# Layer-1 mixture of experts: dense blocks replaced by 79 sorted blocks filled and read back by indirect DMA

## The chip, the core and the metric

The kernel runs on one core of one Trainium2 chip. The metric is the device time of one execution in microseconds, the median of several. PE is the matrix engine, PEld its weight loads, DVE the vector engine, ACT the scalar engine, POOL is GpSimd and SP the engine that issues most DMAs.

## The reference

Two layers act on x, two sequences of 1024 tokens of 128 float32 features. Each layer normalizes x and adds attention and a mixture of experts (MoE), both of the normalized tokens, to x. Layer 0 has sigmoid attention and 32 experts of width 64. Layer 1 has softmax attention with relative positions, 16 heads of 8, and 16 experts of width 176, of which each token uses four, plus a shared expert of width 352:

```python
topk_idx, topk_w = _gate(x, gate_w, gate_bias)
combine_w = (jax.nn.one_hot(topk_idx, E, dtype=x.dtype) * topk_w[..., None]).sum(1)
g = jnp.einsum('th,eih->tei', x, gate_proj)
u = jnp.einsum('th,eih->tei', x, up_proj)
act = jax.nn.silu(g) * u
y = jnp.einsum('tei,ehi,te->th', act, down_proj, combine_w)
sg = x @ shared_gate_w.T
su = x @ shared_up_w.T
y = y + jax.nn.silu(sg) * su @ shared_down_w.T
```

The gate takes a sigmoid of 16 logits, keeps two of four groups of experts, then the four best experts, and normalizes their scores to sum to one. The sum over experts may therefore be taken over all sixteen with zero weights, or over the four chosen ones alone.

## The kernel before

Everything is float32. Tokens are handled in tiles of 128 (NT = 8 a sequence) and in blocks of 512 (TB).

**Layer 0** is a loop over c = 0 to 95 (N_ATT): each step makes the scores of one key tile (scores0, L413) and the weighted values of the step before (values0, L442), and between them opens and closes one FFN unit (open_unit L311, close_unit L336). A unit is 128 hidden rows for 512 tokens: two matmuls into PSUM (L319, L320), a sigmoid on ACT (L325), two multiplications on DVE (L326, L327), one on POOL (L333) by the combine weights of the rows' experts, which SP has spread over the partitions from a DRAM tensor (cb, L317, three buffers), and a third matmul (L345) that adds to the block's output. Every expert is computed for every token.

**Layer 1's FFN** (blocks1, L520) has the same form: 22 units of routed experts (M1 = 16 x 176 / 128) and three of the shared expert for each of four token blocks, 100 units, in the steps from c = 96 on. The gates (gate1, L489) run piecewise on DVE, that of sequence 0 within layer 0 and that of sequence 1 at c = 107 to 124. folded1 (L512) adds a finished block to x2s, the running x. Under these units lies the start of layer 1's attention: projections (L574), operands (L594), the first positions (L613) and ten scans (L652), spread over the steps c = 136 to 190 (L861). SP also writes the zero rows of the bounce tensors there (L558).

**Layer 1's attention** is a loop over 128 steps t: 16 groups of 8, a group being a sequence, a set of heads (s) and a block of 512 queries (q). A step computes scores and exp for one key tile (L705, L730), the values of the step before (L733), and a scan for a step LEAD = 10 ahead, which finds the row maxima that the scores need: four matmul row groups into four PSUM banks, reduced on DVE (L683, L688). positions(n, pair) makes the relative-position terms of two query tiles: matmuls (L624), copies on ACT (L627) and POOL (L629), a write to DRAM (L636) and a skewed read back (near, L642). It is called at step 8n - 13 or 8n - 9, three steps before its first scan. PE's order is the order of the program; POOL's and SP's instructions stand in their queues in the order in which they are issued, and one that waits holds those behind it. After a sequence's last group, finish (L757) and project (L768) write the output.

Of the kernel before, what the change touches and what calls it, by code (L numbers as in the profile page):

```python
# [19 lines left out]
B = 2  # L20
# [14 lines left out]
M1 = E1 * I1 // P  # L35
SH1 = 2 * I1
W = 512
# [5 lines left out]
def fused_layers_kernel(ctx: ExitStack, tc: tile.TileContext, a: dict, out: bass.AP):  # L43
# [13 lines left out]
    const = ctx.enter_context(tc.tile_pool(name="const", bufs=1))  # L57
    moe_pool = tc.tile_pool(name="moe", bufs=2, side="right")
# [28 lines left out]
    w1_pool = tc.tile_pool(name="w1pool", bufs=1, side="right")  # L87
    l1w = w1_pool.__enter__()
# [3 lines left out]
    def load(pool, name, shape, src=None):  # L92
        t = pool.tile(shape, F32, tag=name, name=name)
        nc.sync.dma_start(t, a[name] if src is None else src)
        return t
# [26 lines left out]
    gproj = load(l1w, "gproj", [P, E1 * I1])  # L122
    uproj = load(l1w, "uproj", [P, E1 * I1])
    dproj = load(l1w, "dproj", [P, M1, D], a["dproj"].rearrange("(m p) d -> p m d", p=P))
    sgw = load(l1w, "sgw", [P, SH1])
    suw = load(l1w, "suw", [P, SH1])
    sdw = l1w.tile([P, 3, D], F32, tag="sdw", name="sdw")
# [68 lines left out]

    def layernorm(x, xn, pool):
# [38 lines left out]
    def top_k(work, n_rows, n, k, pool, tag):  # L236

        picked = pool.tile([P, n_rows, n], F32, tag=tag + "p", name=tag + "p")
# [3 lines left out]
        for j in range(k):  # L242
# [6 lines left out]
            if j == 0:  # L249
                one = picked  # L250
            else:
                one = pool.tile([P, n_rows, n], F32, tag=tag + "o", name=tag + "o")
            nc.vector.tensor_tensor(one, eq, spread(best, n), ALU.is_equal)
            if j:
# [102 lines left out]
    cw1_rows = dram.tile([E1, B * T], F32, tag="cw1", name="cw1")  # L357
# [106 lines left out]
    def merged0(b):  # L464
# [6 lines left out]
        xn1[b] = l0.tile([P, T], F32, tag=f"xn{b}", name="xn1")  # L471
# [7 lines left out]
    def rows1(m):  # L479
        lo, end = m * P, (m + 1) * P  # L480
        got = []
        while lo < end:
            e = lo // I1
            hi = min(end, (e + 1) * I1)
            got.append((lo - m * P, hi - m * P, cw1_rows[e]))
            lo = hi
        return got

    def gate1(b):  # L489
# [11 lines left out]
        picked = yield from top_k(sf, NT, E1, K1, l1w, "e1")  # L501
        nc.vector.tensor_mul(picked, picked, sc)
        nc.vector.tensor_reduce(red, picked, AX.X, ALU.add)
        nc.vector.tensor_scalar(red, red, 1e-20, None, ALU.add)
        nc.vector.reciprocal(red, red)
        nc.vector.tensor_tensor(picked, picked, spread(red, E1), ALU.mult)
        yield
        combine_weights_out(picked, E1, l1w, cw1_rows, b)
# [11 lines left out]
    def blocks1(b):  # L520
        parts = [
# [478 lines left out]
```

## Time and profile before

| | |
|---|---|
| median of 3 runs | 1390.44 us (1388.61 to 1393.4) |
| the profiled execution's own time | 1393.02 us |
| its span | 1391.2 us, granted clock 0.987 |
| layer 0, 0 to 433.3 us | 433.3 us |
| layer 1's FFN and the attention's start, to 750.5 us | 317.2 us |
| layer 1's attention, 128 steps, to the end | 640.7 us |
| DMA over the span | 155.71 MB, mean 112 GB/s |

The span runs from the first instruction to the last. Busy time is summed by engine; a group of instructions is listed by line, engine, operation and tile names, with count, busy time, mean ns of one, and the idle time ahead of them with what ended it. A float32 matmul shows as two rows. The queue of a DMA-issuing engine, such as SP's, is not counted as busy.

### The profile page before, as it was taken

How to read it: one execution, taken by the hardware profiler on the slowest of the kernel's cores; microseconds unless marked ns; L12 is line 12 of the kernel's file. 1: busy time of each engine (PE TensorE's matmuls, PEld its weight loads, DVE VectorE, ACT ScalarE, POOL GpSimd, SP SyncE). 2: the span in 40 equal slices, each digit the busy share in tenths (PEclk: the TensorE clock that was granted, in tenths of full speed). 3: DMA queues.
4: the chain of work that ended last, by engine and by line, in shares of the span. 5: the costliest groups of instructions: out<-in, count | busy, mean ns of one | idle time of the engine just before them, and what ended most of it. 6: DMA issues, size and time to landing. Idle time of an engine off the chain costs nothing.

```text
span 1391.2 us, 21725 instructions
## 1 busy us (share of the span) xinstructions
PE 1300.9 (94%) x8080; PEld 548.6 (39%) x8080; DVE 802.5 (58%) x2111; ACT 613.2 (44%) x1051; POOL 290.9 (21%) x323
## 2 busy tenths in 40 slices
PE   5889999989999999989999999999999999999997
PEld 2323233323333434434434444443544444344443
DVE  7863343653334875646674665666567666666653
ACT  3534444535552222222213555555454454555554
POOL 0124243233333434343231001010000100010000
PEclk9999999999999999999999999999999999999999
DMA  8111111111111343255341555535544544554420
GB/s 274 37 43 58 49 58 46 39 38 41 46 52 55 106 114 100 61 173 154 112 131 57 163 158 182 173 125 159 166 136 161 161 165 137 183 160 141 155 92 16
DMA packets 107146, 155.71 MB, mean 112 GB/s; under 512 B 14464, under 2 KB 85760, under 8 KB 106528
## 3 DMA queue, kind: packets, MB, share of 16 engines
q1 hardware_dynamic: 107040, 154.32, 35.5%
q8 instruction: 64, 1.05, 0.3%
q14 instruction: 42, 0.34, 0.1%
HBM read 99.91 MB, written 54.37 MB: 111 GB/s over the span
## 4 chain that ended last, share of the span: by engine, by line
PE 70%; DVE 17%; DMA 5%; ACT 4%; issue 3%; POOL 1%; SPq 0%; DVEq 0%; POOLq 0%; ACTq 0%
PE big L319 10%; PE sm L724 10%; PE big L320 9%; PE ffn L345 8%; PE acc L741 8%; PE sm L663 8%; PE sm L714 5%; PE big L425 4%; PE acc L451 4%; DVE maxima L688 3%; DMA near<-bounce 3%; DVE junk L683 2%; DMA bounce<-rel 2%; DVE h L327 1%; DVE t L326 1%
## 5 line engine op out<-in xcount | busy, mean ns | idle before, releaser
L730 ACT ACTIVATE p<-sm 128x512 f32<-128x512 f32 x512 | 264.7, 606 | 234.0 <-PE sm L724 233.9
L688 DVE TENSOR_REDUCE maxima<-sm 128x1 f32<-128x512 f32 (+3 forms) x472 | 226.5, 502 | 123.0 <-PE sm L663 123.0
L333 POOL TENSOR_TENSOR h<-h,cb 128x512 f32<-128x512 f32 x152 | 193.6, 1274 | 378.9 <-DVE h L331 194.6
L431 ACT ACTIVATE at<-big 128x1024 f32<-128x1024 f32 (+1 forms) x192 | 144.9, 808 | 149.4 <-PE big L425 143.4
L683 DVE CUSTOM_DVE_ANT_0 junk<-sm,near 128x384 f32<-128x384 f32 (+2 forms) x292 | 130.4, 447 | 67.2 <-PE sm L663 53.6
L325 ACT ACTIVATE sg<-big 128x512 f32<-128x512 f32 (+1 forms) x100 | 59.7, 597 | 226.9 <-PE big L320 224.9
L629 POOL COPY rel<-rel 128x512 f32<-128x512 f32 x64 | 37.5, 614 | 537.5 <-ACT rel L627 537.5
L741 PE MATMUL acc<-p,vs 128*32 128x512 f32 (+1 forms) x1288 | 144.6, 518 | 0.4 <-ACT yu L753 0.4
L330 DVE SCALAR_TENSOR_TENSOR t<-big,b,sg 128x512 f32<-128x512 f32 x64 | 47.9, 749 | 157.7 <-ACT sg L329 157.7
L714 PE MATMUL sm<-ident,near 128*128 128x128 f32 x704 | 107.5, 284 | 21.2 <-DVE maxima L683 12.6
L326 DVE TENSOR_TENSOR t<-big,sg 128x512 f32<-128x512 f32 (+1 forms) x100 | 68.9, 689 | 92.0 <-ACT sg L325 91.9
L724 PE MATMUL sm<-qa,kls 32*128 32x512 f32 (+3 forms) x832 | 116.9, 545 | 0.0
L663 PE MATMUL sm<-kls,qs 32*128 32x512 f32 (+2 forms) x776 | 105.0, 569 | 1.2 <-ACT p L730 1.2
L714 PEld LDWEIGHTS sm<-ident,near 128*128 128x128 f32 x704 | 76.8, 142 | 70.9 <-issue 20.0
L425 PE MATMUL big<-qm,xT 32*128 32x512 f32 (+3 forms) x768 | 101.6, 544 | 3.1 <-ACT at L431 1.9
L345 PE MATMUL ffn<-h,dproj 128*128 128x512 f32 x176 | 91.9, 604 | 11.2 <-POOL h L333 11.2
L319 PE MATMUL big<-xT,gproj 128*128 128x512 f32 x176 | 92.3, 606 | 4.4 <-DVE h L327 3.5
L320 PE MATMUL big<-xT,uproj 128*128 128x512 f32 x176 | 90.3, 595 | 0.0
L451 PE MATMUL acc<-at,xn 128*32 128x512 f32 (+3 forms) x768 | 83.9, 510 | 6.5 <-POOL at L436 4.6
L319 PE MATMUL big<-xT,w 128*128 128x512 f32 x128 | 75.2, 670 | 14.9 <-DVE h L331 12.5
L627 ACT COPY rel<-sm 128x512 f32<-128x512 f32 x116 | 59.5, 600 | 50.5 <-issue 49.5
L327 DVE TENSOR_TENSOR h<-big,t 128x512 f32<-128x512 f32 (+1 forms) x100 | 69.1, 691 | 9.3 <-DVE t L326 0.9
(232 smaller groups left out, 1419.8 us busy)
## 6 DMA issues: line engine op xcount, KB each, us to landing
bounce<-rel SPq DMA_DIRECT2D x64, 768.0 KB
near<-bounce SPq DMA_DIRECT2D x64, 768.0 KB
cb<-cw SPq DMA_DIRECT2D x144, 128.0 KB
cb<-cw SPq DMA_DIRECT2D x32, 256.0 KB
cb<-cw SPq DMA_DIRECT2D x16, 224.0 KB
cb<-cw SPq DMA_DIRECT2D x16, 192.0 KB
cb<-cw SPq DMA_DIRECT2D x16, 160.0 KB
bounce<-zeros SPq DMA_DIRECT2D x40, 63.5 KB
```

Of the source, the lines that this page charges most:

```text
L319: nc.tensor.matmul(hh[0:m, 0, :], wa, xT, start=True, stop=True)
L320: nc.tensor.matmul(hh[0:m, 1, :], wb, xT, start=True, stop=True)
L333: nc.gpsimd.tensor_mul(h[0:m], h[0:m], cb[0:m])
L345: nc.tensor.matmul(y, w2m, h[0:m], start=first, stop=last and bias_mm is None)
L425: nc.tensor.matmul(halves[r // 2][:, r % 2, off:TB], xT0[b][g, kt * P:(kt + 1) * P], masked[b, s][g, q * TB + off:(q + 1) * TB], start=Tru ...
L663: nc.tensor.matmul(ps[r][:, (k0 - lo) * P:(k1 - lo) * P], qs[g, qt * P:(qt + 1) * P], (kh if far else kl)[g, k0 * P:k1 * P], start=True, s ...
L683: nc.vector.tensor_tensor_reduce(junk[:, 0:(k1 - k0) * P], part, near[n, i][:, r, w0:w0 + (k1 - k0) * P], 1.0, -BIG, ALU.add, ALU.max, mx[ ...
L688: nc.vector.tensor_reduce(mx[:, r, slot:slot + 1], part, AX.X, ALU.max)
L714: nc.tensor.matmul(ps[r][:, i * P:(i + 1) * P], near[n, i][:, r, w0:w0 + P], ident, is_transpose=True, start=(i == close[0]), stop=False, ...
L724: nc.tensor.matmul(ps[r][:, i0 * P:i1 * P], k[g, kt * P:(kt + 1) * P], qa[n][g, i0 * P:i1 * P], start=(m == 0 and not close), stop=(m == l ...
L730: nc.scalar.activation(p[:, r, :], ps[r], AF.Exp)
L741: nc.tensor.matmul(y[rows_of(r), part], vs[:, kt, rows_of(r)], probs[n, kt][:, r, part], start=(kt == 0), stop=(kt == NT - 1 and part.stop ...
```

## The change

The routed experts of layer 1 are no longer computed for every token. M1's units are gone from blocks1, which keeps the three shared units per block, and the loop of layer 0 ends 22 steps after step 96, with the attention's start in its last 16 steps.

Instead, top_k now hands out each of the four choices by itself (chosen), gate1 keeps the four weights (share), and sort1 gives each token and choice a slot: the tokens of one expert take whole blocks of 128 slots, in the order of the experts, NBLK = 79 blocks in all, which hold any routing of 2048 x 4 choices. It also lists for each block the rows of its expert's weights. gate1 of sequence 1 and sort1 run piecewise in the attention's steps 1 to 25.

Three DRAM tensors are new: slots_x and slots_y (the blocks' inputs and outputs, 79 x 128 rows of 512 B) and wx (for each expert 128 rows of 608 floats: the gate, up and down weights of both halves of its 176 hidden rows). In layer 0's steps 30 to 72 SP writes the bounce tensors' zero rows (moved here), zeros into slots_x (clear) and wx (regroup); gproj, uproj and dproj are no longer loaded to SBUF.

In steps 26 to 57 POOL issues 64 scatters, two a step: 128 normalized tokens each, to their slots. Ahead of step 64, when sequence 0's scores are done, all 79 blocks run on PE (experts): SP fetches four blocks of tokens at a time, PE turns them, POOL gathers each block's weights by an indirect DMA into a ring of six buffers, and hidden and outputs are two blocks apart. In steps 65 to 96 POOL issues 64 gathers of outputs, two a step, and DVE adds each, times its weight, into x2s two steps later. The positions due at step 63 are moved behind the experts, to step 64. The ring of near tiles shrinks from 12 to 10, the output is written from x2s, and project adds into it.

```diff
 SH1 = 2 * I1
+I1H = I1 // 2
+WX = 4 * I1H + 2 * D
+
+NBLK = (B * T * K1 + E1 * (P - 1)) // P
+NTT = B * NT
...
-    gproj = load(l1w, "gproj", [P, E1 * I1])
-    uproj = load(l1w, "uproj", [P, E1 * I1])
-    dproj = load(l1w, "dproj", [P, M1, D], a["dproj"].rearrange("(m p) d -> p m d", p=P))
-    sgw = load(l1w, "sgw", [P, SH1])
...
-            if j == 0:
+            if each:
+                one = each[j]
+            elif j == 0:
...
-    cw1_rows = dram.tile([E1, B * T], F32, tag="cw1", name="cw1")
+    slots_x = dram.tile([NBLK * P, D], F32, tag="slots_x", name="slots_x")
+    wx = dram.tile([E1 * P, WX], F32, tag="wx", name="wx")
+    slots_y = dram.tile([NBLK * P, D], F32, tag="slots_y", name="slots_y")
...
-        xn1[b] = l0.tile([P, T], F32, tag=f"xn{b}", name="xn1")
+        xn1[b] = const.tile([P, T], F32, tag=f"xn1{b}", name="xn1")
...
-        nc.vector.tensor_reduce(red, picked, AX.X, ALU.add)
+        mine = slice(b * NT, (b + 1) * NT)
+        yield from top_k(sf, NT, E1, K1, l1w, "e1", [t[:, mine, :] for t in chosen])
+        for j in range(K1):
+            nc.vector.tensor_mul(sf, chosen[j][:, mine, :], sc)
+            nc.vector.tensor_reduce(share[:, mine, j], sf, AX.X, ALU.add)
+            yield
+        nc.vector.tensor_reduce(red, share[:, mine, :], AX.X, ALU.add)
...
+        nc.vector.tensor_tensor(share[:, mine, :], share[:, mine, :], spread(red, K1), ALU.mult)
...
+        nc.vector.tensor_add(some, chosen[0], chosen[1])
+        nc.vector.tensor_add(some, some, chosen[2])
...
+        nc.vector.tensor_add(some, some, chosen[3])
+        ps = small()
+        rank, in_tile = (ps[:, i * NTT * E1:(i + 1) * NTT * E1] for i in range(2))
+        nc.tensor.matmul(rank, ahead, flat[0], start=True, stop=True)
+        nc.tensor.matmul(in_tile, ones, flat[0], start=True, stop=True)
...
+        nc.vector.tensor_copy(some, in_tile)
+        nc.vector.memset(at[:, 0, :], 0.0)
+        for t in range(1, NTT):
+            if t % 8 == 1:
+                yield
+            nc.vector.tensor_add(at[:, t, :], at[:, t - 1, :], some[:, t - 1, :])
+        nc.vector.tensor_add(n_tok, at[:, NTT - 1, :], some[:, NTT - 1, :])
...
+        nc.vector.tensor_add(at, at, rank)
...
+        nc.vector.tensor_tensor(some, spread(n_tok, NTT), filled.unsqueeze(1).to_broadcast(by_e), ALU.is_gt)
+        nc.vector.tensor_reduce(n_blk, some, AX.X, ALU.add)
...
+        nc.vector.tensor_tensor(some, lower, n_blk.unsqueeze(1).to_broadcast(by_e), ALU.mult)
+        nc.vector.tensor_reduce(start_, some, AX.X, ALU.add)
+        nc.vector.tensor_add(end_, start_, n_blk)
+        nc.vector.tensor_scalar(start_, start_, float(P), None, ALU.mult)
...
+        nc.vector.tensor_tensor(at, at, start_.unsqueeze(1).to_broadcast(wide), ALU.add)
+        for j in range(K1):
+            nc.vector.tensor_mul(some, chosen[j], at)
+            nc.vector.tensor_reduce(slot[:, :, j], some, AX.X, ALU.add)
+            yield
+        nc.vector.tensor_copy(slot_of, slot)
+        row = l1w.tile([P, NBLK], F32, tag="row", name="row")
+        for lo in range(0, NBLK, NTT):
+            n = min(NTT, NBLK - lo)
+            nos = block_no[:, lo:lo + n]
+            nc.vector.tensor_tensor(some[:, 0:n, :], end_.unsqueeze(1).to_broadcast([P, n, E1]),
+                                    spread(nos, E1), ALU.is_le)
+            nc.vector.tensor_reduce(row[:, lo:lo + n], some[:, 0:n, :], AX.X, ALU.add)
+            yield
+        nc.vector.tensor_scalar(row, row, float(E1 - 1), float(P), ALU.min, ALU.mult)
+        nc.vector.tensor_scalar(row, row, row_no, None, ALU.add)
+        nc.vector.tensor_copy(weight_row, row)
...
+    def clear(i):
+
+        n = min(4, NBLK - 4 * i)
+        nc.sync.dma_start(slots_x[4 * i * P:(4 * i + n) * P, :].rearrange("(i p) d -> p i d", p=P),
+                          zeros.unsqueeze(1).to_broadcast([P, n, D]))
...
+    def regroup(i):
+
+
+        by_row = wx.rearrange("(e p) w -> p e w", p=P)
+        if i < 2:
+            nc.sync.dma_start(by_row[:, :, i * I1:(i + 1) * I1],
+                              a[("gproj", "uproj")[i]].rearrange("p (e w) -> p e w", e=E1))
+        else:
+            c = slice(2 * I1 + (i - 2) * D, 2 * I1 + (i - 1) * D)
+            nc.sync.dma_start(wx.rearrange("(e p) w -> e p w", p=P)[:, 0:I1H, c],
+                              a["dproj"].rearrange("(e j p) d -> j e p d", j=2, p=I1H)[i - 2])
+            nc.sync.dma_start(by_row[I1H:P, :, c], zeros[I1H:P].unsqueeze(1).to_broadcast([P - I1H, E1, D]))
...
+    def scatter(i):
+
+        t, j = i // K1, i % K1
+        x = xn1[t // NT][:, (t % NT) * D:(t % NT + 1) * D]
+        nc.gpsimd.indirect_dma_start(
+            slots_x[:, :], bass.IndirectOffsetOnAxis(ap=slot_of[:, t, j:j + 1], axis=0), x, None
+        )
...
+    def gather(i):
+
+        t, j = i // K1, i % K1
+        y = pools["late"].tile([P, D], F32, tag="got", name="got", bufs=6)
+        nc.gpsimd.indirect_dma_start(
+            y, None, slots_y[:, :], bass.IndirectOffsetOnAxis(ap=slot_of[:, t, j:j + 1], axis=0)
+        )
+        fetched[i] = y
+
+    def gathered(i):
+        t, j = i // K1, i % K1
+        x = x2s[t // NT][:, t % NT, :]
+        nc.vector.scalar_tensor_tensor(x, fetched.pop(i), share[:, t, j:j + 1], x, ALU.mult, ALU.add)
+        if t < NT and j == K1 - 1 and t % 4 == 3:
+            result(0, t // 4)
+
+    def result(b, q):
+        nc.sync.dma_start(out[b, q * TB:(q + 1) * TB, :].rearrange("(i p) d -> p i d", p=P),
+                          x2s[b][:, 4 * q:4 * q + 4, :])
+
...
+    def fetch_w(i):
+        if i >= NBLK:
+            return
+        if i % 6 < 4:
+            t = const.tile([P, T], F32, tag=("xn10", "xn11", "xT10", "xT11")[i % 6], name="blockw")
+        else:
+            t = pools["late"].tile([P, 2 * T], F32, tag="p", name="blockw", bufs=2)
+        nc.gpsimd.indirect_dma_start(
+            t[:, 0:WX], None, wx[:, :], bass.IndirectOffsetOnAxis(ap=weight_row[:, i:i + 1], axis=0)
+        )
+        block_w[i] = t
+
+    def fetch_x(g):
+        if 4 * g >= NBLK:
+            return
+        n = min(4, NBLK - 4 * g)
+        t = held["room"][:, g % 2]
+        nc.sync.dma_start(
+            t[:, 0:n, :], slots_x[4 * g * P:(4 * g + n) * P, :].rearrange("(i p) d -> p i d", p=P)
+        )
+        block_x[g] = t
...
+    def turn_x(g):
+        if 4 * g >= NBLK:
+            return
+        n = min(4, NBLK - 4 * g)
+        ps = quads(small())
+        x = block_x.pop(g)
+        for i in range(n):
+            nc.tensor.transpose(ps[:, i, :], x[:, i, :], ident)
+        t = held["room"][:, 2 + g % 2]
+        nc.scalar.copy(t[:, 0:n, :], ps[:, 0:n, :])
+        block_xT[g] = t
+
+    def hidden(i):
+
+        w, xT = block_w[i], block_xT[i // 4][:, i % 4, :]
+        ps = quads(small())[0:I1H]
+        for j in range(4):
+            nc.tensor.matmul(ps[:, j, :], w[:, j * I1H:(j + 1) * I1H], xT, start=True, stop=True)
+        sg = w[0:I1H, WX:WX + 2 * P].rearrange("p (i c) -> p i c", c=P)
+        h = pools["late"].tile([P, 2, P], F32, tag="bh", name="bh", bufs=3)[0:I1H]
+        nc.scalar.activation(sg, ps[:, 0:2, :], AF.Sigmoid)
+        nc.vector.tensor_mul(sg, ps[:, 0:2, :], sg)
+        nc.vector.tensor_mul(h, ps[:, 2:4, :], sg)
+        block_h[i] = h
...
+    def outputs(i):
+        g, n = i // 4, min(4, NBLK - i // 4 * 4)
+        if i % 4 == 0:
+            block_y[g] = quads(small())
+        ps, h, w = block_y[g], block_h.pop(i), block_w.pop(i)
+        for j in range(2):
+            c = 4 * I1H + j * D
+            nc.tensor.matmul(ps[:, i % 4, :], h[:, j, :], w[0:I1H, c:c + D], start=(j == 0), stop=(j == 1))
+        if i % 4 == n - 1:
+            t = held["room"][:, 4 + g % 2]
+            nc.scalar.copy(t[:, 0:n, :], ps[:, 0:n, :])
+            nc.sync.dma_start(
+                slots_y[4 * g * P:(4 * g + n) * P, :].rearrange("(i p) d -> p i d", p=P), t[:, 0:n, :]
+            )
...
+    def experts():
+
+        held["room"] = pools["l1"].tile([P, 2 * NG * NEAR], F32, tag="rel", name="room").rearrange(
+            "p (k i c) -> p k i c", k=6, c=D)
+        for g in range(2):
+            fetch_x(g)
+        turn_x(0)
+        for i in range(NBLK + 2):
+            if i < NBLK:
+                hidden(i)
+            if i >= 2:
+                outputs(i - 2)
+                fetch_w(i + 4)
+            if i % 4 == 1:
+                turn_x(i // 4 + 1)
+                fetch_x(i // 4 + 2)
...
     def blocks1(b):
-        parts = [
-            (P, gproj[:, m * P:(m + 1) * P], uproj[:, m * P:(m + 1) * P], dproj[:, m, :], None, None,
-             rows1(m)) for m in range(M1)
-        ]
+        parts = []
...
-            slot = 4 * (n % 3) + 2 * pair + j
+            slot = (4 * n + 2 * pair + j) % 10
...
-        nc.vector.tensor_add(o, x2s[b][:, 4 * q:4 * q + 4, :], ps)
-        nc.sync.dma_start(out[b, q * TB:(q + 1) * TB, :].rearrange("(i p) d -> p i d", p=P), o)
+        x = x2s[b][:, 4 * q:4 * q + 4, :]
+        nc.vector.tensor_add(x, x, ps)
+        if b:
+            result(b, q)
...
+    for i in range(N_BOUNCE):
+        at(30 + i, bounce_rows, i)
+    for i in range(-(-NBLK // 4)):
+        at(30 + N_BOUNCE + i, clear, i)
+    for i in range(4):
+        at(60 + 4 * i, regroup, i)
...
     at(N_ATT, blocks1, 0)
     at(N_ATT + 2, added0, 1)
...
+    at(N_ATT + 5, lambda: l0_pool.__exit__(None, None, None))
+    at(N_ATT + 5, opened1)
+    at(N_ATT + 9, turned1, 1)
+    at(N_ATT + 9, blocks1, 1)
+    LAST = N_ATT + 22
...
-                at(N_ATT + 40 + (t - min(begin)) * 58 // -min(begin), f, *args)
+                at(LAST + t * (LAST - N_ATT - 6) // -min(begin), f, *args)
...
+    SORT, SCATTER, EXPERTS = 1, 26, 8 * len(groups) // B
...
+    def routing():
+        yield from gate1(1)
+        yield from sort1()
...
+    for t in range(SORT, SCATTER - 1):
+        for i in range(1 + t % 2):
+            beside(t, route_on)
+    beside(SCATTER - 1, route_on, True)
+    for i in range(NTT * K1):
+        beside(SCATTER + i // 2, scatter, i)
+        beside(EXPERTS + 1 + i // 2, gather, i)
+        beside(EXPERTS + 3 + i // 2, gathered, i)
+    for i in range(4):
+        beside(EXPERTS - 1, fetch_w, i)
...
         for t in range(N_STEPS + 1):
+            if t == EXPERTS:
+                values(t // 8 - 1, NT - 1, whole)
+                for i in range(4, 6):
+                    fetch_w(i)
+                experts()
             before = begin.get(t, ())
+            if t == EXPERTS:
+                before = list(before) + held_back
+            elif t == EXPERTS - 1:
+                held_back = [e for e in before if e[0] is positions]
+                before = [e for e in before if e[0] is not positions]
...
-            if t:
+            if t and t != EXPERTS:
                 values(n, kt, left if halved else whole)
...
+            for f, args in aside.get(t, ()):
+                f(*args)
```

## The prediction

> **What bounds the kernel now.** I read the page's first two parts, then the busy time by stage, the groups of the second stage, PE's timeline, the waits and the chain. The profiled execution took 1393.02 us, its span is 1391.2 us, and the median shown is 1390.44 us; the sum below is made on the span: 1.8 us lie around it, and this execution is 2.6 us above the median, so 0.8 us come off at the end.
>
> ```profile
> PE 1300.9 (94%) x8080; PEld 548.6 (39%) x8080; DVE 802.5 (58%) x2111; ACT 613.2 (44%) x1051; POOL 290.9 (21%) x323
> ```
>
> PE is busy nearly throughout. The stages, cut at the first layer-1 expert matmul (433.3), the first attention score of layer 1 (750.5), the middle of that attention and the end (columns: us, then busy us of PE, PEld, DVE, ACT, POOL, clock, DMA share, GB/s):
>
> ```profile
> 0.00:433.30 433.30, 395.91 (x2041) 132.73 (x2042) 208.06 (x486) 203.74 (x277) 128.04 (x138) 0.98 0.20 64
> 433.30:750.50 317.20, 298.59 (x860) 130.31 (x858) 204.60 (x408) 74.19 (x125) 121.76 (x115) 0.99 0.38 110
> 750.50:1070.50 320.00, 306.04 (x2592) 144.70 (x2596) 198.05 (x625) 168.15 (x325) 22.36 (x38) 0.99 0.49 158
> 1070.50:1391.20 320.70, 300.35 (x2592) 140.82 (x2584) 191.76 (x593) 167.17 (x325) 18.78 (x32) 0.98 0.41 133
> ```
>
> The change empties the second row and puts new work at the third row's end. A step of the attention is 640.7/128 = 5.0 us, PE-bound, with DVE at 62% and POOL at 7%. The expert groups of the second row, and how closely PE packs such matmuls:
>
> ```profile
> L319 PE MATMUL big<-xT,gproj 128*128 128x512 f32 x176 | 92.3, 606 | 4.4 <-DVE h L327 3.5 <-DVE maxima L683 0.9
> L345 PE MATMUL ffn<-h,dproj 128*128 128x512 f32 x176 | 91.9, 604 | 11.2 <-POOL h L333 11.2
> ```
> ```profile
> 557.55 1.05 PE L590 MATMUL big<-wv,xT 128*128 128x128 f32 x8
> 558.44 1.02 PE L319 MATMUL big<-xT,gproj 128*128 128x512 f32 x2
> 559.30 1.02 PE L320 MATMUL big<-xT,uproj 128*128 128x512 f32 x2
> ```
>
> Each fp32 matmul is two rows (88 units, x176). A 512-wide one takes 559.30-558.44 = 0.86 us, and four 128-wide ones, eight rows, 0.89 us: 0.111 us a row. Last, what the attention hangs on besides PE; the chain crosses the position round trip:
>
> ```profile
> 796.08 0.62 POOL rel L629
> 796.70 0.02 issue
> 796.72 4.81 DMA bounce<-rel
> 801.53 0.02 issue
> 801.54 4.92 DMA near<-bounce
> 806.46 0.02 issue
> 806.48 0.56 DVE junk L683
> ```
>
> A copy on POOL, a write, a read, a scan on DVE: whatever delays POOL there has little slack.
>
> **What the Trainium skill says.** (1) "DMA: Bandwidth & Descriptors", section "Anatomy of one DMA — SWDGE (gpsimd) path": a DMA from GpSimd costs about 2.0 us + bytes/436e3. POOL issues no DMA in this trace, so nothing agrees or differs. (2) The same page, "Two DMAs through the same engine are not ordered": a DMA that depends on another must wait for its landing, not only stand behind it. The trace agrees for SP: its near reads wait 179.8 us in total, 64 times, for the bounce writes ahead of them on the same queue. (3) "SBUF — State Buffer", "Who interferes with whom": a DVE instruction with two SBUF inputs blocks against GpSimd ones that read SBUF. It agrees: L255 on DVE takes 0.28 us normally and 1.31 us at 492.58, while L333 runs on POOL.
>
> **The change, part by part.**
>
> *Removed: dense experts.* 88 units of three matmuls, 88 x 3 x 0.86 = 227 us of PE, with their h muls on POOL and cb loads. 12 shared units stay, 31 us. What is late next: the prelude of the attention, which these units covered. Its chain: merging and layernorm of sequence 1 end at 458 as now, turned and projected tokens give the first positions at about 462. The copies (ACT 4 x 0.60, POOL 2 x 0.61), write and read (4.8 + 4.9) bring the first near tile at 475. Ten scans follow on DVE at 3.0 us (L688 and L683 with its accumulator read, 384 us over 128 scans), and negmax, augment, qa take 2.5, so scores start at about 508; with the shared units' muls, 512. PE's own work there (31 for units, some 35 for the rest of the row's groups) fits into 79 us. The stage falls from 317 to 79: **-238 us** (bounds 72 to 95 us for the stage).
>
> *Into layer 0.* 40 zero rows moved forward, 20 clears of 256 KB and six regroup DMAs stand on SP ahead of cb loads. SP mostly waits there for buffers (L317 for POOL h, 472.6 us), landings held POOL up 17.9 us in all, and cb is three deep: **+3** (0 to 15, if a 1.4 MB regroup, some 5 us at the 322 GB/s below, uncovers a cb). The initial loads lose 4.2 MB that nothing waited for: 0.
>
> *Routing moved under attention.* gate1(1) and sort1 add about 110 DVE instructions in steps 1 to 25: some 50 of 0.2 to 0.3 us (gate rows 471 to 501) and about 26 on 256 elements at 0.45, with small ones 29 us. DVE has 1.9 us free per step, so it fits, but sits ahead of scans in order, whose PSUM banks PE waits for; and two ACT table loads (1.28 us). **+12** (3 to 29).
>
> *64 scatters, two per step from step 26, on POOL.* Each names all of slots_x as output, so each must wait for the landing of the one before, and the waiting instruction blocks POOL: the rel copies and the whole near round trip stand behind it. Price of one, issue to landing: the page gives 2.0 + 65.5 KB/436e3 = 2.15 us; the nearest trace row, bounce<-rel, 4.8 us for 768 KB among the same traffic. I take 3.0. Two plus a rel copy's share (0.3) are 6.3 us per 5.0 us step: **+42** over 32 steps (0 at the lower price, 157 at the upper).
>
> *The experts.* NBLK = 79 blocks, whatever the routing. PE per block: hidden 8 rows and outputs 4 at 0.111, turning 2 rows at 0.12 (the chain has twelve such transposes in 1.46): 1.58 us. ACT: a 256-wide sigmoid 0.38 and half of a 0.60 copy, 0.68. DVE: two 256-wide muls at 0.42, 0.84. DMA: weights 128 x 2432 B = 311 KB, x and y 65.5 KB each, 442 KB; the trace moves 158 GB/s at a share of 0.49, so 322 at full: 1.37 us. The weight ring: fetch_w(i+4) waits for outputs(i-2), and hidden(i+4) comes three iterations later, so an iteration is at least a third of a gather: 2.71 us by the page, 4.9 like near: 0.9 to 1.6 us. Everything is below PE, but three of them closely; I take 1.8 us (1.58 to 2.5): 142. Fill, drain and the table loads add 8, and the positions held back to step 64 lose one of three steps of lead, 5. **+155** (130 to 215).
>
> *64 gathers and weighted adds.* DVE 64 x 0.3 = 19 us over 32 steps, in its free time but ahead of scans: 6; gathers ahead of the rel copies on POOL, four groups, 1.5 us: 6. **+12** (3 to 30). Removing o and adding in x costs 0.
>
> Sum: -238 + 3 + 12 + 42 + 155 + 12 = -14, span 1377, median **1376 us**.
>
> **The rivals.** *B, slower: making indirect descriptors on POOL is the bound.* If each index costs POOL time, a scatter with its landing takes 3.5 us: (7.3 - 5.0) x 32 = 74; the weight gathers pace a block at 2.0: 158 + 13 = 171; gathers 15, the rest as above: -238 + 3 + 12 + 74 + 171 + 15 = +37, **1427 us**. It decides from about 3.1 us a scatter and 1.9 a block: 48 + 163 + 12 + 12 + 3 = 238, all that the first term saves. For it: no POOL DMA is in the trace, and one per 1.6 us is asked. Against: POOL has nothing else to do, 7% busy. *C, faster: scatters don't wait for each other*, or land in 2.2 us, and the 5 us step hides them: 42 becomes 5, **1339 us**. For it: writes to distinct rows need no order. Against: the output is named whole. *D, it does not do what it says*: 79 blocks are fixed and the dense units are gone by code, so the work does fall; I give it no chance of its own.
>
> **How the numbers follow.** Forecast (A) 0.40, B 0.38, C 0.22. A measurement of this kernel can tell about 0.3% from no change. A's own spread crosses that band a little: faster 0.31 + 0.21 from C = 0.52; same 0.07; slower 0.03 from A, 0.37 from B, 0.01 from C = 0.41. Range: C with blocks at 1.65 us, 12 us less, gives 1327; B with a scatter at 3.8 us adds 19, 1446. So 1325 to 1445; of the faster cases alone, 1325 to 1385.
>
> **What would show it.** Scores starting near 512 us prove the first term. In steps 26 to 58, POOL waiting for its own DMA and steps of 6.3 us prove the scatter term; steps of 5.0 us prove C. In the expert stretch, PE close to 90% busy at 1.6 to 1.8 us a block proves my price; POOL nearly always issuing, PE waiting for the weights, proves B. I am wrong if the prelude takes much over 95 us, or if an indirect DMA is far from 3 us.

## The result and the profile after

The change makes the kernel slower: 1474.32 us median (1472.44 to 1480.09, 4 runs) against 1390.73 us (1388.61 to 1393.4), ratio 1.0607 with a 95% interval of 1.0572 to 1.0642. The forecast was 1376 us, in a range of 1325 to 1445. The profiled execution took 1480.09 us, its span is 1478.4 us at a mean granted clock of 0.917 (0.987 before).

The engines' line, the chain by line and the expert group of the page of the kernel after:

```profile
PE 1237.3 (84%) x8567; PEld 581.1 (39%) x8567; DVE 773.8 (52%) x2211; ACT 617.8 (42%) x1086; POOL 379.7 (26%) x450
...
DMA slots_x<-xn,slot_of 11%; PE sm L930 7%; PE acc L948 6%; PE sm L869 6%; POOL blockw L648 4%; PE sm L920 4%; DVE maxima L894 3%; DMA near<-bounce 3%; DVE junk L889 2%; DMA got<-slots_y,slot_of 2%; DMA bounce<-rel 2%; ACT p L937 1%; DMA blockw<-wx,weight_row 1%; PE sm L829 1%; ACT rel L833 1%
...
L680 PE MATMUL sm<-room,blockw 128*88 128x128 f32 x632 | 83.1, 275 | 15.7 <-DMA blockw<-wx,weight_row 14.5
```

PE fell from 94% to 84% of a longer span: PE got less work, as planned, and stands still for 241 us in place of 90. The landing of scatters leads the chain, the sequence of work that ended last, with 11% of the span, some 160 us. The two dense groups of 92 us each are gone; the largest of the experts' groups has 83.1 us. The same view by stage, with the columns that the prediction used. The rows are layer 0, the FFN and the attention's start, the first half of the attention in three pieces (routing, scatters, rest), the experts, and the second half in two (gathers, rest):

```profile
0.00:431.30 431.30, 396.30 (x2034) 132.00 (x2035) 206.50 (x489) 203.77 (x277) 129.77 (x146) 0.98 0.28 82
431.30:520.30 89.00, 73.97 (x309) 34.20 (x307) 63.75 (x175) 21.26 (x36) 10.45 (x27) 0.90 0.33 107
520.30:617.00 96.70, 86.94 (x674) 42.42 (x674) 68.08 (x242) 45.87 (x85) 4.74 (x8) 0.90 0.41 131
617.00:811.50 194.50, 105.36 (x832) 47.53 (x832) 67.71 (x212) 53.23 (x103) 71.26 (x78) 0.77 0.28 90
811.50:973.00 161.50, 144.03 (x1183) 67.23 (x1183) 96.78 (x306) 77.25 (x150) 14.82 (x24) 0.93 0.52 166
973.00:1109.00 136.00, 120.53 (x1042) 115.08 (x1045) 68.17 (x164) 53.25 (x120) 70.04 (x75) 1.00 0.79 242
1109.00:1215.00 106.00, 64.90 (x419) 29.31 (x413) 52.69 (x158) 27.73 (x53) 64.56 (x70) 0.71 0.43 135
1215.00:1478.40 263.40, 245.28 (x2089) 113.36 (x2085) 150.07 (x470) 135.45 (x263) 14.06 (x24) 0.97 0.38 123
```

Against the stages of before: layer 0 -2.0 us, FFN stage 89.0 in place of 317.2, so -228.2, first half of the attention 452.7 in place of 320.0, so +132.7, experts +136.0, second half 369.4 in place of 320.7, so +48.7. The sum is +87.2, which is 1478.4 - 1391.2. (The prediction's cut at 1070.5 us lies two steps early: 249 exponentials, four to a step, start before it, and the scores of step 64 start at 1079.4. Cut there, the halves before are 328.8 and 311.9 us, and the change costs them +123.9 and +57.5.) What was to be saved was saved, and the experts were cheaper than forecast. The loss is in the two rows where row moves run: in 617 to 811.5 PE does 20 steps in 194.5 us, 9.7 us each, and is idle for 89 us; in 1109 to 1215 it is idle for 41.

In GpSimd's timeline of the kernel after, two pairs of rel copies with what stands between them (start, duration, instruction, idle time before it and what ended it):

```profile
627.08 1.17 POOL L835 COPY rel<-rel 128x512 f32<-128x512 f32 x2
628.41 1.23 POOL L611 DMA_INDIRECT slots_x<-xn,slot_of  x1 [0.17 <-issue]
635.77 0.96 POOL L611 DMA_INDIRECT slots_x<-xn,slot_of  x1 [6.13 <-DMA slots_x<-xn,slot_of]
...
672.26 0.96 POOL L611 DMA_INDIRECT slots_x<-xn,slot_of  x1 [1.53 <-DMA slots_x<-xn,slot_of]
674.75 0.96 POOL L611 DMA_INDIRECT slots_x<-xn,slot_of  x1 [1.53 <-DMA slots_x<-xn,slot_of]
675.71 1.17 POOL L835 COPY rel<-rel 128x512 f32<-128x512 f32 x2
```

Between two pairs, which the program sets four steps apart, stand sixteen scatters and not eight: only PE is kept in program order in this loop, and the order of the other engines' instructions, fixed when the kernel is built, put them together. Each scatter waits for the landing of the one before, 1.5 us as a rule and 6.1 where a bounce write has just been issued. A copy of vs, the values of one set of heads, stands there too, in the lines left out. So 48.6 us pass between these two pairs (43.8 to 46.3 between the next ones) in place of 20. What that does further on, in the timeline of all engines:

```profile
686.36 0.42 DVE L889 CUSTOM_DVE_ANT_0 junk<-sm,near 128x256 f32<-128x256 f32 x1 [31.69 <-DMA near<-bounce]
...
687.18 1.90 PE L930 MATMUL sm<-qa,khs 32*128 32x512 f32 x2 [29.22 <-DVE maxima L894]
```

The scan on DVE waits 31.7 us for its near tile, and PE 29.2 us for the maxima. The waits of the whole execution (total us, times, longest):

```profile
POOL slots_x L611 <- DMA slots_x<-xn,slot_of: 120.8, 62, 6.1
DVE junk L889 <- DMA near<-bounce: 105.1, 11, 31.7
...
DVE x L629 <- DMA got<-slots_y,slot_of: 47.3, 38, 6.7
```

The position round trip of the chain shown before is thus the way by which GpSimd's queue reaches PE. The last line, weighted adds that wait for gathers, is a second way, met below.

### The profile page after: what moved, and what is told of

Its sections match the earlier page's. It is cut to its first block, busy times and chain, and to the rows that moved or that the text cites. A ratio compares the mean times of both kernels' runs of the same rounds, so it can differ in the third digit from the quotient of the medians.

```text
span 1478.4 us, 23014 instructions
## 1 busy us (share of the span) xinstructions
PE 1237.3 (84%) x8567; PEld 581.1 (39%) x8567; DVE 773.8 (52%) x2211; ACT 617.8 (42%) x1086; POOL 379.7 (26%) x450
## 4 chain that ended last, share of the span: by engine, by line
PE 27%; DMA 18%; DVE 9%; issue 8%; POOL 6%; ACT 2%; POOLq 0%; DVEq 0%; ACTq 0%; SPq 0%
DMA slots_x<-xn,slot_of 11%; PE sm L930 7%; PE acc L948 6%; PE sm L869 6%; POOL blockw L648 4%; PE sm L920 4%; DVE maxima L894 3%; DMA near<-bounce 3%; DVE junk L889 2%; DMA got<-slots_y,slot_of 2%; DMA bounce<-rel 2%; ACT p L937 1%; DMA blockw<-wx,weight_row 1%; PE sm L829 1%; ACT rel L833 1%
## 5 line engine op out<-in xcount | busy, mean ns | idle before, releaser
L948 PE MATMUL acc<-p,vs 128*32 128x512 f32 (+1 forms) x1288 | 152.8, 545 | 0.4 <-ACT yu L960 0.4
L930 PE MATMUL sm<-qa,kls 32*128 32x512 f32 (+3 forms) x832 | 127.2, 589 | 18.8 <-DVE maxima L894 18.8
L355 POOL TENSOR_TENSOR h<-h,cb 128x512 f32<-128x512 f32 x64 | 83.3, 1302 | 193.8 <-DVE h L353 183.6
L869 PE MATMUL sm<-kls,qs 32*128 32x512 f32 (+2 forms) x776 | 110.6, 582 | 1.8 <-DVE at L560 1.5
L611 POOL DMA_INDIRECT slots_x<-xn,slot_of x64 | 62.5, 976 | 144.3 <-DMA slots_x<-xn,slot_of 120.8
L930 PE MATMUL sm<-qa,khs 32*128 32x512 f32 (+3 forms) x512 | 67.9, 525 | 36.5 <-DVE maxima L894 36.5
L648 POOL DMA_INDIRECT blockw<-wx,weight_row x79 | 74.8, 947 | 88.2 <-PE sm L695 49.2
L680 PE MATMUL sm<-room,blockw 128*88 128x128 f32 x632 | 83.1, 275 | 15.7 <-DMA blockw<-wx,weight_row 14.5
L829 PE MATMUL sm<-posd,qs 32*128 32x256 f32 x464 | 61.5, 428 | 35.0 <-DVE maxima L889 22.2
L680 PEld LDWEIGHTS sm<-room,blockw 128*88 128x88 f32 x632 | 71.7, 157 | 20.4 <-PE sm L695 9.7
```

The source lines that it names most:

```text
L648: nc.gpsimd.indirect_dma_start(t[:, 0:WX], None, wx[:, :], bass.IndirectOffsetOnAxis(ap=weight_row[:, i:i + 1], axis=0))
L680: nc.tensor.matmul(ps[:, j, :], w[:, j * I1H:(j + 1) * I1H], xT, start=True, stop=True)
L869: nc.tensor.matmul(ps[r][:, (k0 - lo) * P:(k1 - lo) * P], qs[g, qt * P:(qt + 1) * P], (kh if far else kl)[g, k0 * P:k1 * P], start=True, s ...
L930: nc.tensor.matmul(ps[r][:, i0 * P:i1 * P], k[g, kt * P:(kt + 1) * P], qa[n][g, i0 * P:i1 * P], start=(m == 0 and not close), stop=(m == l ...
L948: nc.tensor.matmul(y[rows_of(r), part], vs[:, kt, rows_of(r)], probs[n, kt][:, r, part], start=(kt == 0), stop=(kt == NT - 1 and part.stop ...
```

## The experiments

Three ideas were to be told apart. **T1**: the order in a queue; moves stand, bunched, ahead of instructions on which the attention hangs. **T2**: the landing waits between scatters, whatever the order. And a remainder: routing, contention, clock. Each run is cut as follows (us): the start, to the first exponentials of layer 1; the first half, to the first expert matmul; the experts, to the next exponentials; the second half, to the end. The spans are those of the profiled executions. e3, e4, e7 and e11 leave out part of the work: they price something and are no candidates.

| kernel | start | first half | experts | second half | span | median, ratio to before (95%) |
|---|---|---|---|---|---|---|
| after | 525.6 | 447.4 | 136.1 | 369.3 | 1478.4 | 1474.32, 1.0607 (1.0572 to 1.0642) |
| e1 | 525.2 | 401.8 | 139.3 | 412.0 | 1478.3 | 1481.35, 1.0666 (1.0633 to 1.0699) |
| e2 | 525.5 | 408.1 | 138.1 | 387.0 | 1458.7 | 1460.75, 1.0505 (1.0477 to 1.0533) |
| e3 | 528.1 | 423.0 | 134.3 | 383.5 | 1468.9 | 1471.46, 1.0591 (1.0565 to 1.0616) |
| e4 | 527.7 | 348.1 | 135.3 | 308.2 | 1319.3 | 1321.56, 0.9492 (0.9457 to 0.9527) |
| e5 | 527.3 | 346.6 | 135.1 | 366.7 | 1375.7 | 1377.43, 0.9901 (0.9874 to 0.9927) |
| e6 | 524.3 | 346.3 | 133.9 | 352.8 | 1357.3 | 1362.28, 0.9796 (0.977 to 0.9822) |
| e7 | 530.1 | 355.7 | 136.4 | 409.2 | 1431.4 | 1432.13, 1.0285 (1.0259 to 1.031) |
| e8 | 527.4 | 420.4 | 137.0 | 358.0 | 1442.8 | 1441.11, 1.0345 (1.0316 to 1.0374) |
| e9 | 523.2 | 347.2 | 134.9 | 311.9 | 1317.2 | 1320.16, 0.9514 (0.9483 to 0.9546) |
| e10 | 526.0 | 345.6 | 134.0 | 372.6 | 1378.2 | 1379.74, 0.9937 (0.9918 to 0.9956) |
| e11 | 525.1 | 324.0 | 132.0 | 308.8 | 1289.9 | 1297.41, 0.9354 (0.9326 to 0.9383) |

**e4, nothing moved.** All scatters, gathers and weighted adds are left out.

```diff
-        beside(SCATTER + i // 2, scatter, i)
-        beside(EXPERTS + 1 + i // 2, gather, i)
...
-        nc.vector.scalar_tensor_tensor(x, fetched.pop(i), share[:, t, j:j + 1], x, ALU.mult, ALU.add)
```

> Edit: all 64 scatters, 64 gathers and the weighted adds are left out, so the experts compute on zero rows and their outputs are dropped; routing, experts, weight fetches, clears and regroups stay. What it leaves is the change without its row moves: T1: the attention stands at 5.0 us a step with 17 us for the routing, 431 + 89 + 337 + 136 + 325 = 1318 us. If the routing on DVE, the lost lead after the experts or a lower clock carries a large part of the loss by itself: 1360 us or more.

Measured 1321.56 us. The row moves and the adds, with what waits for them, are the whole loss: 447.4 - 348.1 = 99 us in the first half and 369.3 - 308.2 = 61 in the second. The start and the experts don't change.

**e1, program order on GpSimd.**

```diff
-    with tc.manual_schedule(engines={mybir.EngineType.PE}):
+    with tc.manual_schedule(engines={mybir.EngineType.PE, mybir.EngineType.Pool}):
```

> Edit: GpSimd is added to the engines whose instructions stay in program order in the attention loop, so eight scatters (four steps' worth) stand between two pairs of rel copies, in place of up to 18, and eight gathers in place of up to 29; every landing wait stays. Theory T1 (bunches of scatters and gathers ahead of the rel copies hold up the near tiles): eight scatters at 2.5 us with one or two that take 6 us are some 25 us per 20 us of attention, so the first half loses about 45 us in place of 115, and the gathers, 8 x 1.25 us per 20 us, about 10 in place of 49: 1474 - 70 - 39 = 1365 us, the longest idle of PE under 12 us. Rival T2 (the 64 landing waits cost their own time whatever their order): 1465 to 1480 us.

Measured 1481.35 us: T1, as I had it, missed, and the time is about what T2 said. But the halves do not stay as they were, as T2 had it. The first gained, 447.4 to 401.8, and the second lost as much, 369.3 to 412.0. There the gathers now stand behind rel copies that wait, and the adds on DVE, whose order is not held, wait 90.2 us for gathers, where they waited 47.3. GpSimd's timeline of this run, one period of four steps:

```profile
713.90 1.17 POOL L835 COPY rel<-rel 128x512 f32<-128x512 f32 x2
715.23 0.99 POOL L611 DMA_INDIRECT slots_x<-xn,slot_of  x1 [0.16 <-issue]
722.36 0.96 POOL L611 DMA_INDIRECT slots_x<-xn,slot_of  x1 [6.14 <-DMA slots_x<-xn,slot_of]
...
741.57 1.17 POOL L835 COPY rel<-rel 128x512 f32<-128x512 f32 x2
```

Eight scatters now, as the program has it, but from pair to pair it still takes 27.7 us, where four steps need 20: eight periods lose some 60 us, and the first half stands 54 above e4. Order alone is not enough while every scatter waits.

**e3 and e7, fewer landing waits.** The choices go to four tensors in turn; the experts read only the first, so the inputs of three choices are left out. e7 is this with e1's edit.

```diff
+    slots_by = [slots_x] + [dram.tile([NBLK * P, D], F32, tag=f"slots_x{j}", name=f"slots_x{j}") for j in range(1, K1)]
...
-            slots_x[:, :], bass.IndirectOffsetOnAxis(ap=slot_of[:, t, j:j + 1], axis=0), x, None
+            slots_by[j][:, :], bass.IndirectOffsetOnAxis(ap=slot_of[:, t, j:j + 1], axis=0), x, None
```

> Edit: the scatters of the four choices go to four tensors in turn, and the experts read only the first (so three choices' inputs are left out); a scatter then waits for the landing of the fourth before it, not of the one before. The scheduler bunches them more: 15 and 30 scatters ahead of a pair of rel copies. T2 (the landing waits): a scatter is 0.95 to 1.25 us in place of 2.5, the first half loses its 115 us: 1474 - 105 = 1370 us, and the second half keeps its 49. T1 (bunches times pace): 30 x 1.25 = 38 us per bunch still hold up near tiles, so about half of the 115 us stays: 1415 to 1430 us.

Measured 1471.46 us, which neither expected. A scatter does take 1.26 us now (0.96 and 0.30 to the next), but in the built order the last 49 stand in one row: GpSimd issues them from 641 to 706 us without a rel copy, and PE is busy for 5.4 us between 660 and 700. The edit changed the order as well, so by itself it tells little.

> Edit: GpSimd in program order, as in the first run, and four slot tensors in turn, as in the third (three choices' inputs left out): eight scatters of 1.26 us and two pairs of copies, some 13 us, per 20 us of attention. T2a (given the order, the landing waits are what the first half pays): first half 350 to 358 us in place of 402; the second half has the same gathers as the first run and stays at 412: 525 + 355 + 138 + 412 = 1430 us. If waits don't matter once the order is right, the first half stays at 400: 1475 us.

Measured 1432.13 us, first half 355.7: as T2a expected, 8 us above the kernel without moves. With the order held, the landing waits are worth 401.8 - 355.7 = 46 us of the first half. The second half stays at 409, as it should. In the first half T1 and T2 are thus one product: how many moves stand ahead of a rel copy, times how long each holds the queue.

**e2 and e5, take the others out of GpSimd's queue.** e2 moves the rel tail copies to ACT; e5 moves the vs copies and memsets to DVE too.

```diff
-            nc.gpsimd.tensor_copy(
+            nc.scalar.copy(
                 rel[:, j, :, 2 * RAD:NEAR],
...
-        nc.gpsimd.tensor_copy(vs, v)
+        nc.vector.tensor_copy(vs, v)
...
-        nc.gpsimd.memset(ones, 1.0)
+        nc.vector.memset(ones, 1.0)
```

> Edit: the two tail copies of each rel tile move from GpSimd to ScalarE, so that no step of the near tiles stands behind a scatter or a gather; scatters and gathers keep their order and waits. T1: the scatter stretch runs at the pace of the routing-free attention, 5.0 to 5.2 us a step, the gather stretch too; ScalarE gains 126 copies of about 0.6 us over 128 steps, 0.6 us a step, and has the room (60% busy): 1474 - 110 - 45 = 1320 us, below the kernel before. T2: the landing waits lie on the path by themselves (fetched weights and experts wait for them): 1460 us or more. If the loss is DVE's (the routing and the weighted adds ahead of scans), also 1450 or more.

Measured 1460.75 us, far from 1320 and at T2's figure. Yet between 640 and 780 us PE is busy for about 19 of each 20 us, although the scatters wait longer than before (150.8 us in all). Then this, in the stage view and the timeline of e2:

```profile
780.00:838.00 58.00, 0.00 (x0) 0.00 (x0) 0.00 (x0) 0.00 (x0) 22.67 (x25) 0.54 0.08 26
```
```profile
836.42 0.98 POOL L648 DMA_INDIRECT blockw<-wx,weight_row  x1 [1.55 <-DMA slots_x<-xn,slot_of]
837.40 1.05 POOL L811 COPY vs<-vf 128x1024 f32<-128x1024 f32 x1
838.49 0.58 ACT L796 COPY vf<-sm 128x512 f32<-128x512 f32 x1 [63.29 <-POOL vs L811]
```

PE, DVE and ACT stand still for 58 us until a vs copy on GpSimd has its turn, behind the remaining scatters. Without this piece the first half is 350. So it is not the landing waits by themselves, as T2 has it: I had overlooked the second tenant of the queue.

> Edit: besides the rel tail copies (on ScalarE), the copies and memsets of vs move from GpSimd to VectorE, so that GpSimd issues only scatters, weight fetches and gathers; their order and waits stay. In the run with the rel copies alone moved, all engines but GpSimd stood still for 59 us in one piece while a vs copy waited behind the scatters. T1a (whatever shares GpSimd's queue with the moves waits for them): that piece goes, the first half falls from 408 to about 355 us (348 without any move); the second half, where weighted adds wait for gathers in VectorE's own queue ahead of scans, stays at 380 to 390: 525 + 355 + 138 + 385 = 1403 us. If the scatters' traffic itself slowed the attention (contention), the first half stays over 390 us and the time over 1440.

Measured 1377.43 us, 1% less than the kernel before. The first half is 346.6, that of e4, with all 64 scatters and their waits in place: for the first half T1a is shown, and contention by the scatters' traffic is not seen. No run moves the copies without the row moves, so a small gain from the moving itself could hide a small cost of the scatters; PE idles for 23 us of this half in e5 as in e4, which bounds such a gain. The stage view of e5, its two halves:

```profile
527.30:873.90 346.60, 323.59 (x2673) 153.02 (x2667) 233.24 (x764) 191.96 (x369) 67.81 (x70) 0.97 0.50 165
...
1009.00:1375.70 366.70, 309.47 (x2500) 141.87 (x2494) 203.81 (x631) 176.97 (x342) 60.90 (x64) 0.91 0.40 127
```

The second half remains: PE is idle there for 57 us, in the first for 23.

**e8, e6, e10, e9: the second half.** e8 keeps DVE in program order too, beside GpSimd and PE (e1 otherwise).

> Edit: VectorE too is kept in program order in the attention loop, with GpSimd and TensorE; nothing else. Each weighted add then stands two steps behind its gather and no scan stands behind more than two of them. T1b: the second half falls from 412 (GpSimd alone in order) to about 335 us, the first stays near 400 (the landing waits): 525 + 400 + 138 + 335 = 1398 us. If the second half's loss is the gathers' own place in GpSimd's queue, it stays above 390: 1455 us or more. VectorE in program order may cost by itself, up to 20 us.

Measured 1441.11 us. The second half falls from 412.0 to 358.0, where 335 was expected; the first rises by 19, which was to be allowed for. The adds' wait for gathers, 90.2 us in e1, is gone from the list of waits. So DVE's order, in which the weighted adds stand, counts, but it is not all. e6 is e5 with the adds moved to GpSimd, and with e1's edit, so that they stand in program order there:

```diff
-        nc.vector.scalar_tensor_tensor(x, fetched.pop(i), share[:, t, j:j + 1], x, ALU.mult, ALU.add)
+        y = fetched.pop(i)
+        nc.gpsimd.tensor_scalar(y, y, share[:, t, j:j + 1], None, ALU.mult)
+        nc.gpsimd.tensor_add(x, x, y)
```

> Edit: as the run before, and the weighted adds move from VectorE to GpSimd (a multiply and an add each), where they stand in program order four gathers behind their own. Neither GpSimd's nor VectorE's queue then has a scan or a near tile behind a wait for a move. T1b (two queues: GpSimd's in the first half, VectorE's in the second): both halves come close to the run without moves: 525 + 355 + 138 + 315 = 1333 us, under the kernel before. If gathers, their traffic or GpSimd's reads beside VectorE's slow the second half by themselves, it stays over 350 us and the time over 1370.

Measured 1362.28 us; the second half is 352.8, not 315, while the first stays at 346.3. SP's timeline of e6 shows a third queue:

```profile
1018.09 0.36 SPq L850 DMA_DIRECT2D near<-bounce  x1
1046.46 0.38 SPq L636 DMA_DIRECT2D out_dram<-x  x1
1046.93 1.04 SPq L844 DMA_DIRECT2D bounce<-rel  x2
1051.73 3.68 SPq L850 DMA_DIRECT2D near<-bounce  x2
```

A result write of sequence 0 waits for its sixteen adds, and the bounce writes stand behind it on SP; the scan's wait for near is then 21.2 us. e9 is e6 with these writes issued from GpSimd, and e10 has the same edit on e5, adds on DVE:

```diff
-        nc.sync.dma_start(out[b, q * TB:(q + 1) * TB, :].rearrange("(i p) d -> p i d", p=P),
+        (nc.sync if b else nc.gpsimd).dma_start(out[b, q * TB:(q + 1) * TB, :].rearrange("(i p) d -> p i d", p=P),
```

> Edit: as the run in which GpSimd issues only moves, the weighted adds still on VectorE, and the result writes of sequence 0 issued from GpSimd. T1b (VectorE's queue, with adds that wait for gathers ahead of scans, is the main cause in the second half): little changes, second half 355 to 367, 1368 to 1378 us. If SP's queue was the cause and VectorE's only went along: second half 315 to 325, 1330 us.

> Edit: as the run with the weighted adds on GpSimd, and sequence 0's four result writes are issued from GpSimd, behind the adds they need, and no longer from SP, where one waited for the adds ahead of the bounce writes (TensorE stood still for 18 us twice, VectorE waiting for near). T1c (a third queue, SP's, carries the rest of the second half's loss): second half 352.8 to 315 us, 1362 - 37 = 1325 us. If the gathers slow the second half otherwise: 1355 to 1365.

e10 measured 1379.74 us, e9 1320.16. With the adds on DVE it gains nothing to clear SP (366.7 and 372.6, a little above what T1b said), with SP blocked it gains 14 us to clear DVE, and both together give 311.9, within 4 us of no moves at all. GpSimd's program order came with the adds in e6 and e9 and was not tried apart. DVE's timeline of e10 shows what the adds do there:

```profile
1080.72 0.16 DVE L897 TENSOR_REDUCE negmax<-maxima 128x4 f32<-128x12 f32 x1
1087.70 1.65 DVE L629 SCALAR_TENSOR_TENSOR x<-got,share,x 128x128 f32<-128x128 f32 x5 [6.82 <-DMA got<-slots_y,slot_of]
...
1106.02 0.35 DVE L629 SCALAR_TENSOR_TENSOR x<-got,share,x 128x128 f32<-128x128 f32 x1 [0.93 <-DMA got<-slots_y,slot_of]
1106.29 0.55 DVE L889 CUSTOM_DVE_ANT_0 junk<-sm,near 128x384 f32<-128x384 f32 x1
```

After the negmax at 1080.7 and up to 1106.3 DVE runs nothing but 19 weighted adds of about 0.35 us, with waits for gathers to land between them, and the next scan stands behind them: 25 us in which PE gets no maxima. The built order of DVE has bunched the adds, as that of GpSimd bunched the moves.

**e11, no routing either.** As e4, and without gate1(1) and sort1; the weight rows are constants.

> Edit: as the run without scatters and gathers, and without the routing of sequence 1 and the sort; the 79 weight rows are constants (all blocks fetch expert 0's weights). It prices the routing under the attention, forecast at 12 us: if the first half's 348 us against 320 in the kernel before is the routing on VectorE, it falls to 322 and the time from 1321 to 1297 us; if it is the attention's start with short lead and a lower clock, it stays above 338, 1311 us or more. The layer-0 part, 525 us to the first exponentials, stays.

Measured 1297.41 us. The first half is 324.0: the routing under the attention costs 348.1 - 324.0 = 24 us.

**The version that beats both** is e9. Its engines' line, its second half in the stage view and the wait between its scatters:

```profile
PE 1211.7 (92%) x8567; PEld 574.4 (44%) x8567; DVE 756.6 (57%) x2163; ACT 651.4 (49%) x1150; POOL 406.9 (31%) x500
...
1005.30:1317.20 311.90, 291.94 (x2500) 137.08 (x2494) 184.25 (x567) 176.45 (x342) 136.51 (x194) 0.98 0.47 149
...
POOL slots_x L611 <- DMA slots_x<-xn,slot_of: 185.8, 63, 6.6
```

It does all the work of the change and takes 1320.16 us, 0.9514 of the kernel before (0.9483 to 0.9546), no more than e4, which leaves the moves out: its 64 scatters still wait 185.8 us for each other, but nobody else does. They only just fit, however: the last is issued at 863.1 us, SP's first read of the blocks' tokens waits for its landing until 865.3, and PE turns these tokens at 869.1. Much longer waits would hold up the experts.

## Why the prediction was wrong

Step by step, against the terms of its sum:

- **Dense experts, -238**: measured -228. The stage is 89.0 us where 79 was forecast, within its bounds. Right. (The 384 us of scans belong to 118 of the 128. With all of them, 413.5 us, one takes 3.2 us and not 3.0, so ten account for 2 of the 10 us.)
- **Layer 0, +3**: measured -2. Right.
- **Routing, +12**: 24 us (e4 against e11), within 3 to 29. The mechanism is right, the size half.
- **Scatters, +42**: 99 us (after against e4). This step failed, and not mainly by its price: issue and wait come to (62.5 + 120.8)/64 = 2.86 us a scatter, where 3.0 was taken. The scatters are through in 194.5 us, where 32 steps of 6.3 make 202; but only 20 steps of attention ran beside them. What failed is "64 scatters, two per step from step 26": I read the order from the loop, and on GpSimd the built order is another, sixteen between two pairs of rel copies. With the program's order (e1) the first half stands 54 us above e4. A scatter costs (63.3 + 150.7)/64 = 3.3 us there, where the attention beside it moves on, and the step's own sum then gives (2 x 3.3 + 0.3 - 5.0) x 32 = 61. So of the 57 us missed, by an estimate from e1, some 12 are the price and the remaining 45 the order. It also failed to name the second tenant behind the scatters, the vs copies (58 us in e2).
- **Experts, +155**: 136. The hidden matmuls run from 973.0 to 1104.8, 79 blocks at 1.67 us, where 1.8 was taken, so this term was a little too large; PE is busy for 120.53 of the 136 us, 89%, as foretold for this price.
- **Gathers and adds, +12**: 61 (after against e4). This step failed too. It priced the adds as 19 us of DVE time in its free time, and the gathers ahead of a rel copy at 1.5 us a group. It gave no price to the adds' waiting in DVE's queue ahead of scans for gathers to land, nor to the result writes on SP behind the adds. e9 shows that without these the second half pays 4 us.

The two failed terms miss by 99 - 42 = 57 and 61 - 12 = 49, together 106; the others by +10, -5, +12 and -19, together -2. That is 104, where the span missed by 1478.4 - 1377 = 101; the rest is about what the second half of e4, 308.2, gains on that of the kernel before, 311.9. Neither of the two signs of being wrong that the prediction set came up: the prelude took 89 us and a scatter 2.86. What it named to prove the scatter term came true by half: GpSimd waits for its own DMA, but the steps take 9.7 us and not 6.3.

Rival B ended on the right side, for a wrong reason: GpSimd's issue of an indirect DMA is 0.95 us and no bound, with 1.67 us a block and GpSimd busy for 70.04 of the experts' 136 us, 51%. Rival C's 1339 us lies 19 above what e9 reached, but by luck: C let the waits go, and e9 keeps them all.

Part of the idle costs twice. In 780 to 838 of e2, where PE has no instruction, the granted clock is 0.54. The Trainium skill says in "TensorE: Matmul & The Clock Gate", section "What's actually happening", that after an idle window of some 3.4 us PE's clock falls to half until it has been busy again; the trace agrees with the half, the window's length was not tried. What it costs here is small: PE is busy for 105.36 us in the 20 scatter steps, at a clock of 0.77, where the prediction's row of 320.0 us before, at 0.99, holds 62 steps and so has 306.04/62 = 4.9 us a step, 99 in 20. So some 6 of the 94 us by which the scatters' row exceeds 20 steps of 5.0 are slower matmuls, an estimate from these two rows.

## What to carry to other kernels

When a change puts waiting instructions on an engine, read the built order of every queue that they pass, not the order of the loop, and list who else lives there: here GpSimd (rel and vs copies), DVE (scans) and SP (bounce writes). The scatters' waits cost next to nothing here once nobody else used their queue (e9), and 58 us in one piece where one copy of the critical path still stood in it (e2), so move the tenants before you try to shorten the wait. Clear all the queues together: in the second half two of the three cleared (e6, e10) gained at most 369.3 - 352.8 = 17 us of 61, all three 57. Whether GpSimd's had to be cleared for that half, once DVE's and SP's are, was not tried.

## What the runs showed of the hardware

An indirect DMA of 128 rows takes GpSimd 0.95 us, for rows of 512 B (976 ns mean for a scatter) as for 2432 B (947 ns); free of waits, the next starts 0.30 us later. A scatter lands 2.2 us after its issue in the median, close to the estimate of 2.15 us from the Trainium skill's page "DMA: Bandwidth & Descriptors", section "Anatomy of one DMA — SWDGE (gpsimd) path" (2.0 us + bytes/436e3), but 2.9 us in e9, where the attention keeps its pace beside it. It took up to 7.1 us, and the longest landings go with bounce writes of 768 KB: all four waits above 5 us in the kernel after follow a scatter issued within 1 us of a pair of them. The weights' gather took 4.1 us in the median, where the same estimate says 2.71.
